# Second-layer expert weights: four neighbouring rows to a partition, first weights read with a column stride of four

## The chip, the cores and the metric

The kernel runs on one core of a Trainium2 chip. The metric is the device time of the whole program in microseconds. Several runs of a kernel are taken and their median is compared; one further execution is taken with the hardware profiler, and that one gives the trace.

## The reference

All data are fp32. The input x is 16 sequences of 256 tokens with 128 features (4096 tokens). Two layers follow each other, and each is an attention and a mixture of experts, with a residual and a layer norm behind both.

```python
x = _layernorm(x + _L0_attn_ref(x, ...))   # RMS norm, 16 heads of 64, softmax over 256 keys
x = _layernorm(x + _L0_ffn_ref(x, ...))    # 8 routed experts, hidden 256, top 2, and a shared one
x = _layernorm(x + _L1_attn_ref(x, ...))   # 16 heads of 8, attention among the heads of one token
x = _layernorm(x + _L1_ffn_ref(x, ...))    # 8 experts, hidden 512, top 2
```

The change lies in the last of the four. There, for each token, a router takes the two best of eight experts, and with their probabilities w:

```python
for eid in range(e):
    w = jnp.sum(jnp.where(idx == eid, vals, 0), axis=-1)
    h = jax.nn.gelu(x_flat @ w1[eid].T, approximate=False)   # 128 -> 512
    y = h @ w2[eid].T                                        # 512 -> 128
    out = out + w[:, None] * y
```

## The kernel before, in words

**Layout.** Tokens lie in eight groups of 512 in SBUF (`xg`), each as four chunks of 128 tokens. A group, or half a group for the last one, is a part. The last 256 tokens take a dense way through the experts of both layers (`sequence`, `dense`, tiles `wd`, `ph_d`, `po_d`); all others are routed.

**Routing and lists.** Parts are gathered into waves (`WAVES`: five for layer 0 and three for layer 1). `route` computes for each token and each of its two experts a row number, such that all rows of one expert lie together and each tile of 128 rows belongs to one expert. `send` (L905) scatters the tokens to those rows in DRAM by indirect DMAs from POOL. `lists` then runs over the tiles of a wave, four at a time (a quad): 39, 23 and 19 tiles in layer 1, 81 together. Finally `gathered` (L934) brings two result rows back for each token.

For each quad, `lists` has strands that run beside each other:

- `loads_rows` (L1014) loads 4 x 128 token rows (`xq`), and `turns` (L1060) transposes them into `xqT`.
- `loads_first` (L1039) loads for each tile its expert's first weights into `wa`. In layer 1 these are 128 x 512 values, 256 KB, one partition for each input feature, with the 512 hidden units side by side in 2 KB.
- `loads_second` (L1048) loads in layer 1 the second weights into `wb`. The matrix in DRAM is 512 x 128 (a row for each hidden unit, 512 B). `second` gives the view of it: chunk c of the tile holds the hidden units 128c to 128c+127, one to a partition. Partition p so gets the rows p, 128+p, 256+p and 384+p.
- `firsts` (L1098) multiplies. For each tile and each of the `nh` = 4 chunks of 128 hidden units, `wa[:, c, :]` is the stationary operand (128 features x 128 hidden units) and `xqT` the moving one; the product `ph` has hidden units on partitions and tokens in columns. `gelu` (L1071) takes it to `h`.
- `seconds` (L1118) multiplies `h` chunk by chunk with `wb[:, c, :]` and sums the four in PSUM (`po_e`). The sum over hidden units runs over partitions and chunks, so `h` and `wb` must number the hidden units alike.
- `stored` (L1136) copies the result out and writes it to DRAM.

In layer 0 the hidden size is 256 and `nh` is 2; there one tile `wa` holds both the first and the second weights, and L1035 uses `second` too.

**Order.** The program is written out as one list of instructions by a planner in the kernel. Each strand is a generator that gives the time from which its next step can go, by the planner's own clocks and cost constants (`work`, `moved`), and `everything` always takes the step that is due first. The costs are constants of the source, so the order of the instructions on each engine follows from these numbers and not from the hardware. All plain DMAs are issued from SP, in that order. POOL issues the indirect ones. Buffers are rings; when attention of layer 0 is over (`"over"`), the lists get more buffers (`LATE`).

Each fp32 matmul shows in the trace as two weight loads (PEld, LDWEIGHTS) and two matmul records, while a transpose shows as one of each.

Of the kernel before, what the change touches and what calls it, by code (L numbers as in the profile page):

```python
# [15 lines left out]
P = 128  # L16
# [21 lines left out]
def two_layers(  # L38
# [189 lines left out]
    def work(e, us, *after, ports=False, one=None, mode=P):  # L228

        at = max(clk[e], floor[0], *after)  # L230
        if ports and pool[0] - 0.15 > at:
            us += min(pool[0] - 0.15 - at, pool[1])
        clk[e] = (paced(at, us, mode) if e == "PE" else at + us) + SETUP[e]
        if one is not None:
            pool[:] = clk[e], one
        return clk[e] + 0.08
# [7 lines left out]
    def opened(tag):  # L244

        ends[tag].append(INF)
        return tag, len(ends[tag]) - 1
# [60 lines left out]
    def key(what, w=0, i=0):  # L308

        rank, time = KEYS[what]  # L310
        return (time, rank, w, i)
# [5 lines left out]
    def begin(steps, key):  # L317
        st = Strand(steps, key)
        if st.due is not None:
            strands.append(st)  # L320
# [648 lines left out]
    def lists(r):  # L969


        layer, w = r.layer, r.wave
# [9 lines left out]
        hidden = (HC0, HC1)[layer] * P  # L982
        nh = hidden // P
        w1, w2 = (w1_0, w2_0) if layer == 0 else (w1_1, w2_1)
        w1 = w1.rearrange("e d h -> (e d) h")
        w2 = w2.rearrange("e h d -> (e h) d")
# [4 lines left out]
        xqs, was, wbs, hs, xTs = {}, {}, {}, {}, {}  # L991
# [11 lines left out]
            )  # L1003

        def second(e):
            return w2[bass.ds(e * hidden, hidden), :].rearrange("(c p) d -> p c d", p=P)

        def loads_rows():
# [11 lines left out]
        def loads_first():  # L1020
            for i in range(N):
                if yields and i > 0 and urgent:
                    yield (lambda: INF if downs[0] < i else 0.0), None
                    held.remove("lists")
                    yield (lambda: INF if urgent or "lists" in held else 0.0), None
                    held.append("lists")
                for q in range(number[i]):

                    ring = WB if q % 2 and layer == 0 else WA
                    yield (lambda: max(r.listed, ring.free())), "SP"  # L1030
                    free = ring.free()
                    e = expert_of(starts[i] + q)
                    wa, k = ring.tile([P, 4, P], "wa")
                    if layer == 0:
                        nc.sync.dma_start(out=wa[:, 2:4], in_=second(e))  # L1035
                        at = moved(131072, r.listed, free, us=0.9)
                        wbs[i, q] = wa[:, 2:4], k, at
                        wa = wa[:, 0:2]
                    nc.sync.dma_start(out=wa.rearrange("p c h -> p (c h)"), in_=w1[bass.ds(e * P, P), :])  # L1039
                    was[i, q] = wa, k, moved(131072 * (1 + layer), r.listed, free, us=0.45 + 0.4 * layer)  # L1040

        def loads_second():
            for i in range(N):
                for q in range(number[i]):
                    yield (lambda: INF if (i, q) not in was else WB.free()), "SP"
                    free = WB.free()
                    wb, k = WB.tile([P, 4, P], "wb")
                    nc.sync.dma_start(out=wb, in_=second(expert_of(starts[i] + q)))  # L1048
                    wbs[i, q] = wb, k, moved(262144, free, us=0.85)
# [18 lines left out]
        def gelu(i, qs, place, ph, h, at):  # L1068
            yield max(at, r.weighed if layer == 0 else 0.0), "ACT", "gelu"
            if layer == 1:  # L1070
                nc.scalar.activation(h[:, 0], ph[:, 0], AF.Gelu)  # L1071
                done = function(0.62, "gelu", at)
            else:
                for q in qs:
                    for c in range(nh):
                        b = r.bias[:, starts[i] + q, c : c + 1]
                        nc.scalar.activation(h[:, q - qs[0], c, :], ph[:, q - qs[0], c, :], AF.Gelu, bias=b)  # L1077
                done = function(0.36 * nh * len(qs), "gelu", at, r.weighed)
            closed(place, done)
            for q in qs:  # L1080
                gelued[i, q] = done

        def firsts():
            for i in range(N):
                n = number[i]
                for q0 in range(0, n, per):
                    qs = range(q0, min(n, q0 + per))
                    yield (
                        lambda: INF
                        if i not in xTs or any((i, q) not in was for q in qs)  # L1090
                        else max(xTs[i][2], H.free(), *(was[i, q][2] for q in qs))
                    ), "PE", "m"
                    place, free = opened("m"), H.free()
                    ph = ps_m.tile([P, per, nh, P], FP, tag="m", name="ph")
                    h, k = H.tile([P, per, nh, P], "h")
                    for q in qs:
                        for c in range(nh):
                            nc.tensor.matmul(  # L1098
                                ph[:, q - q0, c, :], was[i, q][0][:, c, :], xTs[i][0][:, q, :], start=True, stop=True
                            )  # L1100
                    at = work("PE", 0.233 * nh * len(qs), xTs[i][2], free, *(was[i, q][2] for q in qs))
                    for q in qs:
                        hs[i, q] = h[:, q - q0], k
                        if layer:
                            WA.done[was[i, q][1]] = at
                    begin(gelu(i, qs, place, ph, h, at), key("w gelu", w))
                XT.done[xTs[i][1]] = at
# [37 lines left out]
        if layer:  # L1145
            begin(loads_second(), key("w loads", w))
        begin(turns(), key(f"w turns {layer}", w))
        begin(firsts(), key(f"w firsts {layer}", w))
        begin(seconds(), key(f"w seconds {layer}", w))
        yield (lambda: 0.0 if len(r.stored) == N else INF), None  # L1150
# [513 lines left out]
```

## Time and profile before

| what | value |
|---|---|
| median of 3 runs | 1212.02 us (1209.06 to 1213.38) |
| the profiled execution, its own time | 1245.39 us |
| its span, first to last instruction | 1243.7 us |
| granted TensorE clock, mean | 0.943 |
| PE busy | 1109.0 us, 89% of the span |
| DMA queue q1 (issued from SP) | 179410 packets, 115.27 MB |
| loads of wb | 81 of 256 KB |
| loads of wa in layer 1 | 81 of 256 KB |

The profiled execution is slower than the median run, so sums over its trace are made against its own 1245.39 us. A row of instructions is read as line, engine, operation, result and operands, shapes, count, then busy time and mean duration in ns, then idle time of the engine before them and what ended it. "PEld" is the weight load, which can overlap the matmul. The chain of waits is the path of work that ended last; shares in it are shares of time. Matmul records overlap, so their durations are latencies, and the pace is read from how long a row of them takes.

### The profile page before, as it was taken

The page shows a single profiled execution, that of the slowest core. Times are in us where ns is not written, and L with a number is a line of the kernel's source. Part 1 is how long each engine was busy: PE and PEld are TensorE (multiplying, and loading weights), DVE is VectorE, ACT ScalarE, POOL GpSimd, SP SyncE. Part 2 cuts the span into 40 slices and gives each one's busy share as a digit, 9 for nine tenths or more (in the row PEclk, how much of TensorE's full clock was granted, in tenths as well). Part 3 has the DMA queues.
Part 4 walks back from the last instruction along what each step waited for, and adds up shares of the span by engine and source line. Part 5 has one row for each costly group of instructions (what it writes and reads, how often), then busy time and mean ns, then how long its engine had stood idle before and what let it go on. Part 6 is the DMA issues. An engine that isn't in the chain of part 4 may idle for free.

```text
span 1243.7 us, 22712 instructions
## 1 busy us (share of the span) xinstructions
PE 1109.0 (89%) x7336; PEld 814.5 (65%) x7336; DVE 900.2 (72%) x1811; ACT 706.0 (57%) x2050; POOL 705.7 (57%) x1089
## 2 busy tenths in 40 slices
PE   9999999979999999999998899987838896797883
PEld 5566667665665666766655677655738795697883
DVE  5767675478878888754877998888878795793433
ACT  5556566476665667676674687653544552342432
POOL 4434372557555468524769557767873546446666
PEclk9999999989999999999999999987888897798997
DMA  8900023430000021151003240135458874684952
GB/s 260 270 1 1 1 86 111 132 106 14 1 5 1 1 63 58 35 145 45 18 4 100 80 133 21 29 119 164 144 162 232 257 230 129 197 245 125 288 177 70
DMA packets 187208, 132.47 MB, mean 107 GB/s; under 512 B 12745, under 2 KB 171474, under 8 KB 187090
## 3 DMA queue, kind: packets, MB, share of 16 engines
q1 hardware_dynamic: 179410, 115.27, 31.6%
q0 software_dynamic: 7680, 15.74, 4.1%
q8 instruction: 59, 0.97, 0.3%
q14 instruction: 59, 0.48, 0.1%
HBM read 97.94 MB, written 33.03 MB: 105 GB/s over the span
## 4 chain that ended last, share of the span: by engine, by line
PE 66%; DVE 11%; POOL 8%; issue 6%; ACT 4%; DMA 2%; SPq 1%; ACTq 0%; DVEq 0%; POOLq 0%
PE s L574 9%; PE po L612 9%; PE t L591 9%; PE po_e L1118 6%; PE ph L1098 6%; POOL rows L905 5%; PE py L629 4%; PE pv L528 4%; PE pq L510 4%; PE pk L510 3%; DVE qk_prod L1216 2%; DMA xq<-rows 2%; PE po_d L1541 1%; POOL pr L558 1%; DVE sc L1220 1%
## 5 line engine op out<-in xcount | busy, mean ns | idle before, releaser
L558 POOL TENSOR_SCALAR pr<-pr,rs 128x256 f32<-128x256 f32 x512 | 253.0, 511 | 220.6 <-DVE rs L554 136.7
L543 ACT ACTIVATE pr<-s,nm 128x256 f32<-128x256 f32 x512 | 235.5, 474 | 26.1 <-DVE nm L537 23.0
L537 DVE TENSOR_REDUCE nm<-s 128x4 f32<-128x1024 f32 x128 | 156.1, 1220 | 58.0 <-PE s L574 53.2
L905 POOL DMA_INDIRECT rows<-x,r_pi x120 | 130.7, 1089 | 58.6 <-DVE r_pi L853 24.4
L934 POOL DMA_INDIRECT y<-outs,r_pi x120 | 120.0, 1000 | 65.8 <-issue 27.4
L612 PE MATMUL po<-pT,v 128*64 128x256 f32 x1024 | 146.0, 397 | 7.2 <-ACT h L1077 3.1
L1098 PE MATMUL ph<-xqT,wa 128*128 128x128 f32 x1028 | 132.8, 287 | 16.6 <-issue 14.2
L591 PE MATMUL t<-ident,pr 128*128 128x128 f32 x1024 | 144.4, 283 | 0.8 <-ACT h L1077 0.8
L591 PEld LDWEIGHTS t<-ident,pr 128*128 128x128 f32 x1024 | 115.7, 145 | 42.4 <-POOL pr L558 20.6
L1098 PEld LDWEIGHTS ph<-xqT,wa 128*128 128x128 f32 x1028 | 126.9, 202 | 22.6 <-issue 16.8
L270 DVE COPY pT<-t 128x512 f32<-128x512 f32 x163 | 106.8, 686 | 42.2 <-PE t L591 38.3
L574 PEld LDWEIGHTS s<-kT,qT 64*128 64x128 f32 x896 | 77.1, 186 | 84.2 <-issue 73.1
L574 PE MATMUL s<-kT,qT 64*128 64x256 f32 x896 | 127.0, 402 | 0.0
L1292 POOL TENSOR_TENSOR av_prod<-sc,qkv 128x1024 f32<-128x1024 f32 x35 | 89.9, 2577 | 50.7 <-ACT sc L1254 35.3
L272 ACT COPY oT<-po 128x256 f32<-128x256 f32 x99 | 36.9, 373 | 130.6 <-PE po L612 119.6
L612 PEld LDWEIGHTS po<-pT,v 128*64 128x64 f32 x1024 | 65.1, 137 | 67.6 <-issue 18.9
L543 ACT ACTIVATION_READ_ACCUMULATOR pr<-s,nm 128x1 f32 x512 | 105.5, 206 | 0.0
L1118 PE MATMUL po_e<-wb,h 128*128 128x128 f32 x648 | 84.3, 292 | 5.5 <-issue 5.5
L1118 PEld LDWEIGHTS po_e<-wb,h 128*128 128x128 f32 x648 | 82.6, 209 | 5.3 <-issue 4.8
L1216 DVE TENSOR_TENSOR qk_prod<-qkv 128x1024 f32<-128x1024 f32 x64 | 82.8, 1294 | 1.8 <-ACT qkv L272 1.8
L1267 DVE TENSOR_REDUCE o<-av_prod 128x64 f32<-128x1024 f32 x62 | 73.3, 1200 | 11.3 <-POOL apart L904 9.7
L1220 DVE TENSOR_REDUCE sc<-qk_prod 128x128 f32<-128x1024 f32 x64 | 78.1, 1220 | 2.2
(233 smaller groups left out, 1971.0 us busy)
## 6 DMA issues: line engine op xcount, KB each, us to landing
wa<-in_w_dram SPq DMA_DIRECT2D x190, 128.0 KB
wa<-in_w_dram SPq DMA_DIRECT2D x81, 256.0 KB
wb<-in_w_dram SPq DMA_DIRECT2D x81, 256.0 KB
xq<-rows SPq DMA_DIRECT2D x38, 256.0 KB
outs<-yq SPq DMA_DIRECT2D x38, 256.0 KB
rows<-clear SPq DMA_DIRECT2D x3, 1472.0 KB
rows<-clear SPq DMA_DIRECT2D x1, 2496.0 KB
rows<-clear SPq DMA_DIRECT2D x2, 1216.0 KB
```

What stands on the lines that cost most here:

```text
L270: nc.vector.tensor_copy(o, i)
L537: nc.vector.tensor_reduce(nm[u], s, AX.X, ALU.max, negate=True)
L543: nc.scalar.activation(pr[u][:, i, :], s[:, i, :], AF.Exp, bias=nm[u][:, i : i + 1], accum_out=su[u][:, i : i + 1],)
L558: nc.gpsimd.tensor_scalar(pr[u][:, i, :], pr[u][:, i, :], rs[:, i : i + 1], 1.0, ALU.mult, ALU.mult)
L574: nc.tensor.matmul(sc[u][:, j, qc, :], q[part, ts(qc, P)], k[part, :], start=True, stop=True,)
L591: nc.tensor.transpose(t[:, kc, ts(qc, P)], pr[u][:, 2 * j + qc, ts(kc, P)], ident)
L612: nc.tensor.matmul(po[j * DH : (j + 1) * DH, :], vs[g, p // 4, 2 * b + kc][:, ts(h, DH)], pT[u][j][:, kc, :], start=(kc == 0), stop=(kc == 1),
L905: i = nc.gpsimd.indirect_dma_start(out=rows[layer][w][:, :], out_offset=bass.IndirectOffsetOnAxis(ap=r.pos[:, k, c : c + 1], axis=0), in_= ...
L934: nc.gpsimd.indirect_dma_start(out=y, out_offset=None, in_=outs[layer][w][:, :], in_offset=bass.IndirectOffsetOnAxis(ap=r.pos[:, k, c0 + c ...
L1098: nc.tensor.matmul(ph[:, q - q0, c, :], was[i, q][0][:, c, :], xTs[i][0][:, q, :], start=True, stop=True)
L1118: nc.tensor.matmul(po[:, q, :], hs[i, q][0][:, c, :], wbs[i, q][0][:, c, :], start=(c == 0), stop=(c == nh - 1))
L1216: nc.vector.tensor_tensor(m, q3[:, ts(j, HALF)].unsqueeze(2).to_broadcast(full), k3.unsqueeze(1).to_broadcast(full), ALU.mult)
```

## The change

In layer 1, `second` gives another view of the same 512 x 128 matrix: partition p gets the rows 4p, 4p+1, 4p+2 and 4p+3, which are 2 KB side by side in memory. Chunk c of `wb` then holds the hidden units 4p+c. So that `h` has the same numbering, `firsts` takes in layer 1 as its stationary operand every fourth column of `wa`, starting at c. The loads of `wa`, layer 0 and the dense way stay as they are, and so do the planner's costs.

```diff
         def second(e):
+            if layer == 1:
+                return w2[bass.ds(e * hidden, hidden), :].rearrange("(p c) d -> p c d", p=P)
             return w2[bass.ds(e * hidden, hidden), :].rearrange("(c p) d -> p c d", p=P)
...
                     for q in qs:
                         for c in range(nh):
+                            wa = was[i, q][0][:, c, :]
+                            if layer == 1:
+                                wa = was[i, q][0].rearrange("d c h -> d (c h)").rearrange("d (p c) -> d c p", c=nh)[:, c]
                             nc.tensor.matmul(
-                                ph[:, q - q0, c, :], was[i, q][0][:, c, :], xTs[i][0][:, q, :], start=True, stop=True
+                                ph[:, q - q0, c, :], wa, xTs[i][0][:, q, :], start=True, stop=True
                             )
```

## The prediction

> **What bounds the kernel now.** I read the page first, then the chain of waits for the stretch in which layer 1's lists run (925 to 1222 us), then the windows over that stretch, then the groups by form on PE's weight load, and last the few instructions in which an engine already reads with a stride. The page's first rows:
>
> ```profile
> span 1243.7 us, 22712 instructions
> PE 1109.0 (89%) x7336; PEld 814.5 (65%) x7336; DVE 900.2 (72%) x1811; ACT 706.0 (57%) x2050; POOL 705.7 (57%) x1089
> ```
>
> PE is the busiest engine, but 89% is an average over stages. Nothing before 925 us is touched by the change, because layer 0 keeps its loads and its reads. The chain of waits restricted to 925 to 1222 us:
>
> ```profile
> by line: PE po_e L1118 18.8%; PE ph L1098 17.3%; issue 16.4%; PE po_d L1541 5.7%; DMA xq<-rows 4.5%; DVE av_prod L1292 3.6%; PE o_sums L1274 3.6%; PE px L1060 3.4%; SPq L1039 3.0%; PE ph_d L1528 2.6%; DVE o L1267 2.3%; PE py L1346 1.9%; ACT
> ```
>
> So 17.3% of 297 us, 51 us, of the path that sets the end is the very line whose operand the change restrides (ph, L1098), and only 4.5% (13 us) is a DMA (the token rows xq). No wb load stands in this list. The windows say where DMA matters (columns: length, PE, PEld, DVE, ACT and POOL busy, granted clock, DMA share, GB/s):
>
> ```profile
> 0.00:10.00 10.00, 7.64 (x36) 6.48 (x37) 2.30 (x7) 2.83 (x10) 1.75 (x8) 1.00 0.79 257
> 230.00:240.00 10.00, 10.00 (x59) 6.38 (x60) 1.54 (x2) 2.27 (x6) 5.72 (x6) 1.00 0.69 197
> 1150.00:1190.00 40.00, 35.70 (x280) 33.16 (x278) 16.35 (x65) 17.20 (x33) 25.76 (x30) 1.00 1.02 288
> ...
> 925.00:1222.00 297.00, 242.65 (x1804) 230.61 (x1805) 194.65 (x442) 121.55 (x218) 157.94 (x184) 0.88 0.70 205
> ```
>
> Over the whole stretch PE is busy 243 of 297 us and the DMA engines 70%. Only around 1150 to 1190 us are the DMA engines full while PE waits, 4.3 of 40 us.
>
> **The change part by part.** It touches 81 tiles of layer 1. On every engine the instructions and their order stay as they are; two things differ.
>
> *The loads of wb.* Each 256 KB load falls from 512 pieces of 512 B to 128 pieces of 2 KB. The trace has no row that times one load, so I take rates: GB/s over DMA share. Layer 0's lists (230 to 240 us, pieces of 512 B and 1 KB) give 197/0.69 = 285 GB/s at full share; the first 10 us, mostly 4 KB rows, give 257/0.79 = 325. The 81 loads are 21.2 MB: 74 us at 285 and 65 us at 325, so at most 9 us of DMA time goes away, 0.11 us for each load. Here a rule is weighed. The Trainium skill, "DMA: Bandwidth & Descriptors", section Specifications, puts the smallest transfer for line rate at 512 B; by it the pieces were long enough already and the gain is nothing; by the rows it is up to 9 us of DMA time. I follow the rows. What is worth time is what falls where DMA sets the pace: about 20 of the 81 tiles lie in 1150 to 1190 us, 20 x 0.11 = 2 us. Elsewhere it is hidden under PE; the bounds are 0 and -6 us. SP issues as many DMAs as before: the median issue is 373 ns for wb and 345 ns for the wa loads, which have 2 KB pieces or 1 KB ones, so at most 81 x 0.03 = 2 us of SP's queue, which is not on the path; I take 0. What else SP issues behind these loads (xq loads, stores, the wd loads) can only be earlier. Nothing on POOL's queue moves, and no wait is added.
>
> *The weight loads of ph.* Each of the 324 matmuls of layer 1's first product is two weight loads and two matmul records, 648 of each. Their 128 weight columns used to lie side by side and now lie 16 B apart. The trace has no weight load with a stride. First, is there slack? Groups by form, PE's weight load (mean ns is the number after the comma):
>
> ```profile
> L1098 PEld LDWEIGHTS ph<-xqT,wa 128*128 128x128 f32 x1028 | 126.9, 202 | 22.6 <-issue 16.8 <-ACT xqT L272 3.9 <-ACT h L1071 0.4
> L629 PEld LDWEIGHTS py<-wout,oT 128*128 128x128 f32 x448 | 51.1, 192 | 5.0 <-issue 5.0
> L612 PEld LDWEIGHTS po<-pT,v 128*64 128x64 f32 x1024 | 65.1, 137 | 67.6 <-issue 18.9 <-ACT pT L272 4.4 <-DVE pT L270 4.0
> ```
>
> 64 columns take 137 ns and 128 take 192, so a column costs 55/64 = 0.86 ns, and 128 cost 110 ns. And the chain, at full clock:
>
> ```profile
> 973.17 3.57 PE ph L1098 x32
> ...
> 1078.02 3.55 PE o_sums L1274 x32
> ```
>
> 32 records of ph take 3.57 us, 112 ns each. 32 records of o_sums, which stream only 64 columns under a 128-column weight load, take as long, 111 ns. So the weight load alone holds PE to 112 ns: it has no slack, and whatever a stride adds comes through in full. Now the bounds. The moving operand of o_sums is itself read with a stride (16 floats, 64 B): its 64 columns fit in 111 ns, so a strided column costs PE at most 1.73 ns, twice 0.86. The upper end is therefore a load of 222 ns, and 648 x (222 - 112) = 71 us more PE time; the lower end is 0, since a stride fetches no fewer columns and a gain is excluded. The nearest row of a strided read against a plain one of the same size is on DVE: L807 reads both inputs 32 B apart, L849 reads plainly.
>
> ```profile
> L849 DVE TENSOR_TENSOR r_scratch<-r_scratch 128x128 f32<-128x128 f32 x3 | 0.9, 292 | 0.1
> L807 DVE TENSOR_TENSOR both<-r_scratch 128x64 f32<-128x64 f32 x3 | 0.7, 250 | 0.0
> L849 DVE TENSOR_TENSOR r_scratch<-r_scratch 128x64 f32<-128x64 f32 x2 | 0.5, 226 | 0.1
> L807 DVE TENSOR_TENSOR both<-r_scratch 128x128 f32<-128x128 f32 x1 | 0.4, 389 | 0.0
> ```
>
> From 64 to 128 elements the plain one gains 66 ns (1.03 each), the strided one 139 (2.17 each): about double, from few samples. The Trainium skill speaks the same way and against the change ("SBUF — State Buffer", Door 1, the note on cachelines): a partition is read in lines of 16 B, and at least two accesses must hit a line for full rate. At 16 B every weight column opens its own line. The page gives no size and names no engine. By the PE row alone the cost may be 0; by the rule with DVE's ratio it is the doubling. I take the doubling.
>
> Of the 71 us, what lies on the path: the pieces of ph on the chain hold 391 of the 648 records, 391 x 0.11 = 43 us. The other 257 (28 us) run beside waits; PE is idle 54 us of the stretch, some 11 of them around 1030 us in a wait for ACT and DVE that longer PE work fills. I let a third through, 9 us. Sum: +43 +9 -2 = +50 us on the profiled execution's own 1245.4 us (1243.7 us of span and 1.7 around it). That execution is 1.028 times the median of the runs, 1212.0, so +50 there is +48.6 on the median: 1260.
>
> If the cover is gone, all 71 us come through. PE's clock could add to that: at 1067.69 us 32 records of o_sums ran at half pace for 7.09 us without the clock coming up, so a PE that loads for as long as it multiplies may not hold its full clock.
>
> **The rivals.** First, *the stride is free and only the DMA gain is left* (the other side): for it, transposes load 128 weight columns in 145 ns and 9 in 97, 0.40 ns a column, so the read path can run twice as fast as these 0.86 ns columns need; if a line per column costs half of that peak rate, 0.81 ns, the stride hides under 0.86. Then the time is 1212 - 2 = 1210, between 1206 and 1213. It decides if a strided load stays under 192 to 195 ns. Against it stand DVE's rows and the rule. Second, *a part of the doubling*: a load some 30 ns longer, 648 x 0.03 = 19 us, three quarters on the path, -2 for DMA: 1224; nothing in the trace points at a value in between. Third, *the change makes no bigger pieces*: the tile is contiguous in a partition and so are rows 4p to 4p+3 in memory, and the built program has the load as 128 x 512 elements; only its effect on rate is open, and without it the main case is 1262.
>
> **How the numbers follow.** Doubling 0.52 (1260, itself 1240 to 1285); part of it 0.12 (1216 to 1240); free stride 0.36. About 0.3%, 3.6 us, is what a measurement of this kernel tells from no change. Of the free case, somewhat over half would be faster than that (0.20), since a gain of 2 us is the middle and 6 the bound but DMA waits can chain; the rest counts as the same (0.15). Slower takes the doubling and the part, with a shade of the free case: 0.65. The range reaches from 1206, the good end of the free case, to 1284, where 71 us come through.
>
> **What would show it.** Right: in the profile after, the layer 1 form of ph on PE's weight load well above 200 ns (near 300), 32 records of ph near 7 us instead of 3.57 while po_e stays at 3.57, PEld busy in the stretch up by some 70 us, and ph's share of the chain about doubled. The packets of q1 fall from 179410 by 31104 (81 x 384). Wrong: a weight load of ph still at 192 ns. If that is so and the time falls by more than 6 us, DMA held more of the path than these windows show; if the load is long and the time has hardly moved, the idle 54 us of PE took it in.

## The result, and the profile after

The changed kernel takes 1264.9 us (median of 6 runs, 1261.6 to 1266.1) against 1212.1 us (6 runs) for the kernel before beside it: a ratio of 1.043, with a 95% interval from 1.041 to 1.045, or 53 us more. The profiled execution took 1264.3 us, span 1262.6 us. (A ratio and its interval are estimated from all runs and can differ by 0.001 or 0.002 from the quotient of the two medians.)

One thing has to be known before the traces are compared. There are four sets of runs, the last three each on a chip of its own, and the kernel before took 1212 to 1213 us in the first and the last of them and 1245 to 1249 us in the two between. They are called the 1212 us sets and the 1245 us sets here. The trace shown with the prediction (1245.4 us) has the time of a 1245 us set, the trace of after belongs to a 1212 us set. So a second trace of the kernel before is used here, from the other 1212 us set (1212.8 us for that execution, span 1211.1), and called the second trace of before.

The page of after, first rows:

```profile
span 1262.6 us, 22712 instructions
PE 1163.3 (92%) x7336; PEld 875.9 (69%) x7336; DVE 901.1 (71%) x1811; ACT 709.8 (56%) x2050; POOL 702.5 (56%) x1089
...
q1 hardware_dynamic: 148306, 115.27, 30.7%
```

The instructions are as many as before. The packets of q1 fell by 31104, which is 81 x 384. Now the ph line, L1103 in after; one line's instructions, durations as minimum, median and maximum in ns:

```profile
L1103 PEld LDWEIGHTS ph<-xqT,wa x1028: 186/329/338, 195.0 to 1223.4; 128*128 128x128 f32 x172
```

The median weight load was 192 ns before and is 329. The chain of after at full clock (start, length, what):

```profile
960.79 7.46 PE ph L1103 x32
968.68 3.57 PE po_e L1123 x32
```

32 records of ph take 7.46 us, 233 ns each instead of 112, and po_e keeps its 3.57. The windows over the layer 1 stretch say what became of that, first in the second trace of before, then in after (length, busy time of PE, PEld, DVE, ACT, POOL, granted clock, DMA share, GB/s):

```profile
925.00:1270.00 345.00, 228.97 (x1815) 218.19 (x1815) 199.08 (x475) 126.22 (x228) 164.23 (x199) 0.92 0.61 179
```

```profile
925.00:1270.00 345.00, 302.11 (x1815) 294.79 (x1815) 198.78 (x475) 128.52 (x228) 164.99 (x198) 0.93 0.59 178
```

PE is busy 73.1 us longer. (The rows of ph alone are busy 78.9 us in this stretch and then 156.3, so the rest of PE's work is 4 us shorter.) From 925 us to the end of the span there were 286.1 us and are 337.6, so PE's idle time went from 57.1 to 35.5 us: 21.6 us of the longer work went into waits, and 51.5 us lengthened the run. The other engines do what they did. The chain of the same stretch, the second trace of before and then after:

```profile
by line: DMA y<-outs,r_pi 14.9%; issue 6.8%; DVE av_prod L1292 6.3%; DVE o L1267 4.6%; DVE sc L1220 4.5%; DVE qk_prod L1216 4.3%; POOL rows L905 3.4%; PE o_sums L1274 3.3%; PE ph L1098 3.0%; POOL y L934 2.7%; POOL n_r L381 1.7%; DVE n_st L3
```

```profile
by line: PE ph L1103 44.0%; PE po_e L1123 21.0%; PE po_d L1546 5.8%; PE ph_d L1533 4.1%; PE o_sums L1279 3.2%; PE px L1062 2.9%; DVE av_prod L1297 2.0%; PE py L1351 1.7%; PE pqkv L1340 1.5%; DMA y<-outs,r_pi 1.5%; PE pl L734 1.2%; PE t_x L4
```

Before, in this set, the end was set mostly by the gathers y and DVE's attention, and ph was on 3.0% of the chain. Now PE sets it.

### The profile page after: what moved, and what is told of

Its sections match the earlier page's. It is cut to its first block, busy times and chain, and to the rows that moved or that the text cites. A ratio compares the mean times of both kernels' runs of the same rounds, so it can differ in the third digit from the quotient of the medians.

```text
span 1262.6 us, 22712 instructions
## 1 busy us (share of the span) xinstructions
PE 1163.3 (92%) x7336; PEld 875.9 (69%) x7336; DVE 901.1 (71%) x1811; ACT 709.8 (56%) x2050; POOL 702.5 (56%) x1089
## 3 DMA queue, kind: packets, MB, share of 16 engines
q1 hardware_dynamic: 148306, 115.27, 30.7%
## 4 chain that ended last, share of the span: by engine, by line
PE 75%; DVE 11%; POOL 6%; ACT 3%; issue 2%; DMA 2%; SPq 0%; ACTq 0%; DVEq 0%; POOLq 0%
PE ph L1103 14%; PE s L574 9%; PE po L612 9%; PE t L591 9%; PE po_e L1123 7%; POOL rows L905 4%; PE py L629 4%; PE pv L528 4%; PE pq L510 4%; PE pk L510 3%; DVE qk_prod L1221 2%; PE po_d L1546 2%; PE ph_d L1533 1%; DVE sc L1225 1%; PE px L1062 1%
## 5 line engine op out<-in xcount | busy, mean ns | idle before, releaser
L1103 PE MATMUL ph<-xqT,wa 128*128 128x128 f32 x1028 | 205.2, 357 | 2.1 <-ACT xqT L272 1.3
L1103 PEld LDWEIGHTS ph<-xqT,wa 128*128 128x128 f32 x1028 | 200.6, 282 | 5.9 <-ACT xqT L272 3.7
L574 PEld LDWEIGHTS s<-kT,qT 64*128 64x128 f32 x896 | 77.1, 186 | 84.2 <-issue 73.1
L1073 ACT ACTIVATE h<-ph 128x512 f32<-128x512 f32 x81 | 48.2, 596 | 81.9 <-PE ph L1103 81.8
L1123 PE MATMUL po_e<-wb,h 128*128 128x128 f32 x648 | 75.9, 275 | 0.0
```

Source lines behind the costliest of these rows:

```text
L574: nc.tensor.matmul(sc[u][:, j, qc, :], q[part, ts(qc, P)], k[part, :], start=True, stop=True,)
L1103: nc.tensor.matmul(ph[:, q - q0, c, :], wa, xTs[i][0][:, q, :], start=True, stop=True)
L1123: nc.tensor.matmul(po[:, q, :], hs[i, q][0][:, c, :], wbs[i, q][0][:, c, :], start=(c == 0), stop=(c == nh - 1))
```

## The experiments

Each is compared with the kernel before in its own set of runs. A diff is against the changed kernel or the kernel before, whichever is nearer, and three dots stand for what is left out.

**The stride alone.** The new view in `second` is taken out and the column read kept.

```diff
-            if layer == 1:
-                return w2[bass.ds(e * hidden, hidden), :].rearrange("(p c) d -> p c d", p=P)
```

> The first weights are read with the column stride of four, the second weights are loaded as before (512 B pieces); the hidden units of the two products then do not match, so another sum is computed with the same work. Theory: the strided weight load of ph is the whole loss, and the loads of wb gave back 2 us of it: 1212 + 53 + 2 = 1267 us, weight load of ph in layer 1 at 329 ns, 32 records of ph in 7.46 us. Rival (the bigger pieces cause a part of the loss, by holding the DMA engines longer beside the token rows): below 1255 us.

Measured: 1284.4 us against 1245.4, ratio 1.032 (1.027 to 1.038), a loss of 34 to 47 us. The expected number of microseconds was for a 1212 us set and does not apply here. The changed kernel itself has in the other 1245 us set the ratio 1.032 too (1.030 to 1.034, below). So within some 6 us the stride alone costs what the whole change costs. Its weight load has the median 329 ns.

**The loads alone.** The column read is taken out, and the first weights are laid out at launch.

```diff
-        "w1_1": a["L1_ffn_w1"].transpose(0, 2, 1),
+        "w1_1": a["L1_ffn_w1"].transpose(0, 2, 1).reshape(NE, D, P, HC1).transpose(0, 1, 3, 2).reshape(NE, D, P * HC1),
```

> The loads of wb in 2 KB pieces, without the stride: the launch lays out the columns of the first weights so that every fourth one already lies side by side (a change of layout only), and the kernel reads them contiguously. Theory: 0 to 6 us under the kernel before, 1210 us in the middle; weight load of ph back at 192 ns, q1 at about 148300 packets. Rival (bigger pieces hurt): above 1216 us.

Measured: 1245.8 us against 1245.4, ratio 1.000 (0.997 to 1.003). In this kernel the dense way keeps the old numbering of its second weights, so its 256 tokens get another sum. A second version has the numbering matched there too:

```diff
-            nc.sync.dma_start(out=w2, in_=d2[e].rearrange("(c p) d -> p c d", p=P))
+            nc.sync.dma_start(out=w2, in_=d2[e].rearrange("(p c) d -> p c d" if layer else "(c p) d -> p c d", p=P))
```

> As the loads alone, and with the numbering matched everywhere: the columns of layer 1's first weights are laid out at launch so that every fourth lies side by side, the second weights are loaded with rows 4p to 4p+3 to partition p in the lists and in the dense way (89 loads of 2 KB pieces), all reads contiguous. The candidate for a version without the price. Theory after the first look (ratio 1.000 for the loads alone): within 0.3% of the kernel before. Rival (a gain shows where PE waits less for other things): 2 to 6 us under.

Measured: 1212.8 us against 1213.0, ratio 0.9995 (0.9984 to 1.0005), in a 1212 us set. So the pieces of 2 KB are worth 2 us at most there; in the 1245 us set the interval leaves 3.5 us either way. The DMA engines do notice: q1's share of their time falls. Page of the second trace of before, then of the matched loads:

```profile
q1 hardware_dynamic: 179410, 115.27, 32.4%
```

```profile
q1 hardware_dynamic: 145234, 115.27, 31.0%
```

32.4% of 1211.1 us is 392 us, and 31.0% of that kernel's span of 1214.3 us is 376: 16 us of DMA time went away, with the eight loads of the dense way in 2 KB pieces too. It is 10 us by the pages of the first version and of the trace shown with the prediction, and 5 us by those of the changed kernel itself (30.7% of 1262.6 us) and the second trace of before. No saving shows in the program's time, so this DMA time had lain beside other work.

**Stride of two, pieces of 1 KB.** Partition p gets two pairs of neighbouring rows.

```diff
-                return w2[...].rearrange("(p c) d -> p c d", p=P)
+                return w2[...].rearrange("(a p b) d -> p a (b d)", a=2, b=2)
...
-                    nc.sync.dma_start(out=wb, in_=second(expert_of(starts[i] + q)))
+                    nc.sync.dma_start(out=wb.rearrange("p (a b) d -> p a (b d)", a=2), in_=second(expert_of(starts[i] + q)))
...
-                                wa = was[i, q][0].rearrange("d c h -> d (c h)").rearrange("d (p c) -> d c p", c=nh)[:, c]
+                                wa = was[i, q][0].rearrange("d c h -> d (c h)").rearrange("d (a p b) -> d a b p", a=2, b=2)[:, c // 2, c % 2]
```

> A middle way: partition p gets two pairs of neighbouring rows of the second weights (2p, 2p+1 and 256 further), in pieces of 1 KB, and the first weights are read with a column stride of two (8 B), so two columns still lie in one line of 16 B. Theory that the cost comes from opening a new 16 B line for every column, with two in a line being enough: weight load of ph at 192 ns, time 1208 to 1213 us. Rival (cost grows with any step away from contiguous, in proportion to the lines touched: twice as many lines as contiguous against four times): a third of the loss, some 1230 us.

Measured: 1245.0 us against 1245.4, ratio 1.001 (0.9995 to 1.003). The weight load has the median 196 ns. The rival's third of the loss is excluded. (The 1208 to 1213 us expected were again for a 1212 us set.)

**Stride of three, loads of wb as before.**

```diff
+                            if layer == 1:
+                                wa = was[i, q][0].rearrange("d c h -> d (c h)")[:, 0 : 3 * P].rearrange("d (p s) -> d s p", s=3)[:, c % 3]
```

> The first weights are read with a column stride of three (12 B; the four chunks then take overlapping columns, so another sum is computed with the same work), second weights loaded as before. 128 columns lie in 96 lines of 16 B, against 32, 64 and 128 at strides of one, two and four, whose weight loads took 192, 196 and 329 ns. Theory (cost by lines opened, about 1.9 ns each, hidden up to some 64 lines): 82 + 96 x 1.93 = 267 ns, and about half of the loss of stride four. Rival A (a switch at 16 B): 192 to 200 ns and no loss. Rival B (a switch above 8 B): 329 ns and the whole loss.

Measured: a weight load of 261 ns (267 expected, and neither 192 nor 329), and 1263.0 us against 1248.5, ratio 1.011 (1.008 to 1.014). By the load the theory holds; the loss, 10 to 17 us, is about a third of the 40.7 us of stride four in this set, not half. The chains of stride two, then of stride three, at full clock:

```profile
1088.34 3.77 PE ph L1103 x32
```

```profile
1008.23 5.58 PE ph L1101 x32
```

With the 3.57 us of contiguous reads and 7.46 of stride four, a record takes 112, 118, 174 and 233 ns for 32, 64, 96 and 128 lines of 16 B. 64, 96 and 128 lines at 1.82 ns each are 116, 175 and 233: one price for each line opened fits all three, and contiguous reads (58 ns by the same price) hide under the 112 that the load takes anyway. The Trainium skill ("SBUF — State Buffer", Door 1, the note on cachelines) has lines of 16 B and two accesses in a line for full rate, and these four points agree with both. That it is the lines opened which count, and not the bytes spanned, is seen for the moving operand in the prediction's row of o_sums: 64 columns that lie 64 B apart span as many bytes as 256 lines and take 111 ns.

**Stride of four in half of the chunks.**

```diff
-                            if layer == 1:
+                            if layer == 1 and c < 2:
```

> Column stride of four in two of the four chunks of each tile only (the other two contiguous; another sum is computed with the same work), second weights loaded as before: 324 weight loads at 329 ns, 39 us of added PE time instead of 79. Theory (the added time falls evenly on parts of PE's work on and off the path): half of the loss of the whole stride, about 20 us where that is 39. Rival (PE's waits take in the first part of it, and only what is beyond them counts): under 10 us.

In this kernel too the second weights are loaded as before. Measured: 1265.1 us against 1248.5, ratio 1.014 (1.012 to 1.016), 15 to 20 us of the 40.7 of the whole stride in that set. The rival's 10 us is excluded. Stride three adds as much PE time, 648 x 0.062 = 40 us, and loses 10 to 17. So the first half of the longer work costs at most its even share, and the waits take in some of it.

**The moving operand strided instead.** The weights are contiguous, the token columns have the stride.

```diff
+                            xq1 = xTs[i][0][:, q, :]
+                            if layer == 1 and n == QT:
+                                xq1 = xTs[i][0].rearrange("d q p -> d (q p)").rearrange("d (p q) -> d q p", q=QT)[:, q]
...
-                                ph[:, q - q0, c, :], was[i, q][0][:, c, :], xTs[i][0][:, q, :], start=True, stop=True
+                                ph[:, q - q0, c, :], wa, xq1, start=True, stop=True
```

> The weights of ph contiguous again, but the moving operand (token columns) read with a stride of four in all full quads of layer 1, 288 of the 324 matmuls (another sum is computed with the same work); second weights loaded as before. Theory (PE pays for lines on either operand alike): records of ph at 233 ns each, the weight load at 192 or stretched by the wait behind it, and 0.89 of the loss of the strided weights. Rival (only the weight load pays: 64 columns with a stride of 64 B kept the pace of 111 ns): no loss.

Measured: 1284.1 us against 1248.5, ratio 1.029 (1.028 to 1.031); 0.89 of the loss of the whole change in this set (40.7 us) is 36.2, and 35.6 were measured. Its chain:

```profile
1018.74 7.25 PE ph L1102 x32
```

227 ns a record, where contiguous reads take 112: either operand of PE pays for lines.

**A strided weight load under a wide matmul.** In the kernel before, the value projection of layer 0.

```diff
-        nc.tensor.matmul(pv, hT[g][:, ts(c, P)], wv_s[:, ts(half, 512)], start=True, stop=True)
+        nc.tensor.matmul(pv, hT[g].rearrange("d (p c) -> d c p", c=NC)[:, c], wv_s[:, ts(half, 512)], start=True, stop=True)
```

> The kernel before, with one other weight operand strided: the value projection of layer 0 (pv, L528, 64 matmuls, 128 weight loads) reads its weights, the normalised tokens, with a column stride of four, so its rows come out in another order (another result, same work). There the moving operand has 512 columns[...]. Theory (a strided weight load of 233 ns is hidden under the longer matmul before it): weight loads at 329 ns, 4 records of pv still in 1.91 us, time within 0.3% of before. Rival (the price is paid wherever the stride stands): 128 x 0.121 = 15 us more.

Measured: 1212.6 us against 1213.0, ratio 1.0003 (0.998 to 1.002). One line's instructions:

```profile
L528 PEld LDWEIGHTS pv<-wv,hT x128: 307/308/332, 12.3 to 789.2; 128*128 128x128 f32 x128
```

The load is longer (190 ns in the second trace of before, 329 expected) and costs the program nothing that shows: the interval ends at 2.5 us, and the rival's 15 us are excluded. The chains, the second trace of before and then this run:

```profile
21.97 0.86 PE pv L528 x2
```

```profile
22.15 0.86 PE pv L528 x2
```

Two records take 0.86 us, 430 ns each, in both: a strided load, which sets a pace of 233 ns in ph, has room under that. Only the first two groups of four records, at 12 and 16 us, take 2.04 us each instead of the expected 1.91. Over all 128 the matmul records are busy 66.1 us against 65.7.

**The kernels again.** The kernel before in the second and in the fourth set, the changed one in the third; nothing is edited.

> The kernel before, unchanged, for a second trace: the one shown ran 33 us over the median of its runs, with PE waiting 43 us for nothing that the profile names. Theory: that was a slower execution of the same program, and a trace near 1212 us has most of those waits gone while the weight loads and matmul records keep their durations (192 and 275 ns). Rival: profiling itself adds the time, and the second trace is near 1245 us again.

Measured 1246.6 us (runs there: 1245.4). It was not an odd execution, since all 35 runs of this set lie at 1240 to 1255 us, and not the profiling, since the profiled execution of after took 1264.3 us beside runs of 1264.9. Both readings fall: the time goes with the set of runs. Each of the last three sets had one chip, at one time, so whether it is the chip itself or something else at that time was not separated.

> The changed kernel, unchanged, beside the kernel before on this chip. The kernel before took 1212 us on the chip of the first comparison and 1245 us on that of the second, with more waits on PE. Theory: the 79 us of longer weight loads (648 x 0.121) are the same on any chip, and where PE waits more, more of them is taken in: a loss of 35 to 42 us where the kernel before takes about 1245, of 50 to 55 where it takes about 1212. Rival: the loss is a fixed 52 us.

Measured: 1289.2 us against 1248.5, ratio 1.032 (1.030 to 1.034), a loss of 40.7 us (38 to 42). The number holds and a fixed loss of 52 us is excluded, but not for the reason expected, which was that more waits take in more of the longer work. The windows of the kernel before in the second set and of the stride alone on the same chip:

```profile
925.00:1290.00 365.00, 250.08 (x1819) 235.59 (x1817) 200.56 (x475) 125.53 (x229) 170.27 (x200) 0.88 0.59 173
```

```profile
925.00:1290.00 365.00, 307.22 (x1829) 297.56 (x1827) 197.40 (x470) 129.48 (x232) 165.81 (x199) 0.92 0.60 174
```

From 925 us to the ends of the spans (1244.9 and 1279.0 us) PE's idle time fell from 69.8 to 46.8 us. So the waits took in 23 us, hardly more than the 21.6 of the 1212 us sets. What is smaller is the longer work itself: PE's busy time grew by 57 us and not by 73. (The trace shown with the prediction and that of the changed kernel in the third set say much the same: 20 us into waits, 65 us more busy time.) A part of it is ph, which grew by 68 us and not by 77, and the rest is other work of PE, which got shorter while the granted clock rose from 0.88 to 0.92.

A price that does not follow the clock would make ph grow less where it runs more often at half clock. In the trace shown with the prediction, ph around 1041 us ran at a granted clock of 0.50, contiguous:

```profile
1040.90 3.49 PEld L1098 LDWEIGHTS ph<-xqT,wa 128*128 128x128 f32 x16 [11.07 <-issue]
```

In the trace of after, eight strided loads around 933 us ran at 0.50 too (the second row is the window, with the clock):

```profile
932.60 1.94 PEld L1103 LDWEIGHTS ph<-xqT,wa 128*128 128x128 f32 x8 [1.08 <-ACT xqT L272]
```

```profile
932.60:934.60 2.00, 2.00 (x8) 2.00 (x9) 1.93 (x11) 0.00 (x0) 0.11 (x1) 0.50 0.01 3
```

The 16 contiguous loads follow each other at 218 ns. The eight strided ones follow at about 230 (1.94 us less some 0.33 of the last load, over seven), the same as at full clock. So the price of a line does not grow at half clock, and there the stride costs some 12 ns a load instead of 121. How much of the difference between the sets comes from this was not tried by an experiment.

> The kernel before once more, for its time and trace on this chip: the runs of one program were 1212 us on the chip of the first comparison and 1245 to 1249 on two others. Theory: where it takes 1212, the stretches of several us in which PE, ACT and SP stand still together and no engine releases them are missing. Rival: the waits are the same in number and every instruction is longer.

Measured 1212.8 us. The groups of ph's matmul, shown first for the trace of the prediction and then for this one:

```profile
L1098 PE MATMUL ph<-xqT,wa 128*128 128x128 f32 x1028 | 132.8, 287 | 16.6 <-issue 14.2
```

```profile
L1098 PE MATMUL ph<-xqT,wa 128*128 128x128 f32 x1028 | 128.1, 282 | 2.5 <-ACT xqT L272 1.8 <-issue 0.4
```

The waits that nothing releases (14.2 us before ph, one of them 10.9) are all but gone, and the median weight load of ph is 192 ns in both, so the rival falls as far as instructions at full clock go. But the waits are not all of the 33 us: in the stretch from 925 us PE is idle 57.1 us instead of 74.6, and busy 229.0 us instead of 244.1 at a granted clock of 0.92 instead of 0.87. What causes the waits and the lower clock in some sets was not tried and stays open.

## Why the prediction was right or wrong

Right in its main case: slower, by the strided weight load of ph, 1260 us forecast and 1264.9 measured. The signs it named came (load 329 ns, 7.46 us for 32 records, 3.57 for po_e, 31104 packets fewer), except that ph's share of the chain grew to more than the double. Its steps:

- *No slack in the weight load*: right. The longer load sets the pace of ph (112 to 233 ns), and where there is slack (pv) next to nothing shows.
- *The size of the longer load*: 222 ns were forecast, as an upper bound, and 233 measured, +122 instead of +110. The mis-sized term is the 1.73 ns of a strided column, which measured 1.82. It came from o_sums, whose 64 columns fit in 111 ns; at 1.77 ns (227/128, the moving operand's own price) they would take 113, so that row probably stood at the limit itself and was no bound with room in it. Over 648 records the rows of ph grew by 77 us, and all of PE by 73, against 71.
- *Doubling rather than free*: right, and DVE's rows had it right from few samples. The free case put a line at 0.81 ns, and 1.82 were measured.
- *What lies on the path, 43 + 9 us*: the total was near and the reading was not. It took ph's share of the chain from a trace with the time of a 1245 us set (17.3%). Where 1212 us holds, ph is 3.0% of the chain. There the loss is what PE's idle time did not take in: 73.1 of busy time less 21.6 us. In the third set, a 1245 us one, the loss was 40.7 us where the sum said 50. A chain of before shows what sets the end now, not what will set it once a line on PE is twice as long.
- *Scaling by 1.028 to the median*: wrong. The two times were of two sets with different waits and clocks, and the loss is larger at 1212 us (53 us against 41), not smaller. The sum was 9 us too high for its own kind of set, and the step to the median took off 1.4 us where some 12 had to be added. The two errors nearly cancel, so that 1260 came so near is in part luck.
- *-2 us for the loads*: -0.2 us by the medians, between -1.9 and +0.6 by the ratio. The DMA time that goes is of the size reckoned (5 to 16 us by the traces, against 9), but that 2 us of it lie on the path stands at the edge of the interval. The bound of 0 that came from the rule of 512 B was the nearer number for the time, though not for the DMA engines.
- *PE's clock could fall*: it did not, 0.93 in the stretch after and 0.92 before.

## What to carry to other kernels

Before an fp32 operand of PE is read with a stride, count the 16 B lines that it opens: up to 64 lines for 128 columns were close to free here, and beyond that each line cost 1.82 ns. Whether this is paid depends on the matmul beside it: with 128 moving columns the pace of PE paid all of it, under 512 next to none. A layout can be prepared at the launch, as in the matched loads, and then no engine reads with a stride. Here that saved the price, but the larger DMA pieces for which it was done bought no time that could be measured.

## What the runs showed of the hardware that was not expected

- The same program takes 1212 or 1245 us, depending on the set of runs, of which the last three had a chip each. In the traces of 1245 us PE has waits that no engine releases (up to 10.9 us before ph in one, 3.9 in the other), and the granted clock from 925 us is 0.87 to 0.88 instead of 0.92.
- The price of a line does not follow the granted clock: a strided load follows the one before it after 233 ns at full clock and about 230 at half clock, while a contiguous one goes from 112 to 218 ns.
- The moving operand pays for lines nearly as the weights do (227 against 233 ns).
